# The five input combinations of a quad in three tiles instead of one

## The chip, the cores and the metric

The kernel runs on one core of a Trainium2 chip. The metric is device time in microseconds (us) of one execution, lower is better. Before the change the median of three runs is 695.69 us (686.91 to 696.82). One further execution was taken by the hardware profiler; all rows below come from it.

## What is computed

The reference is a StyleGAN-like stack of four modulated 1-D convolutions (kernel size 3, 64 channels in and out) on 128 samples of 64 channels and 1024 points, added to its input. Each sample has its own weights, modulated by its style vector:

```
s = style @ mw.T + mb
weight = SCALE * w * s[:, None, :, None]
demod = rsqrt(sum(weight * weight, axis=(2, 3)) + EPS)
weight = weight * demod[:, :, None, None]
```

The four layers are "same", "upsample" (transposed convolution with stride 2, then a blur), "same" and "downsample" (a blur, then a convolution with stride 2), each with a bias, and `x + layers(x)` is the result. There is no nonlinearity between the layers. So, away from the ends of a row, the four layers and the residual are one convolution per sample. The kernel builds those combined weights for each sample on the chip and applies them; the few points at the two ends of each row are computed separately.

## The kernel before

**Quads.** Four samples are one quad, and 32 quads are worked off in one unrolled loop (`for q in range(NQ)`). A sample fills 64 of the 128 partitions, so a quad is two pairs of samples. The row of 1024 points comes from memory as three planes (point numbers modulo 3), and the combined convolution is done by a Toom-Cook-like scheme: instead of nine products of weight taps with planes, five products, numbered 0 to 4, of five combinations of the weights with five combinations of the input. Each product is 24 matmuls of 64x64 weights with 340 points.

**Input side.** For each quad VectorE first makes `in3` (the combination for product 3, from the loaded planes X alone), then the helper tile G in three instructions (`in_g01` twice, `in_g2`). From G, GpSimd makes `in1` and `in2` (products 1 and 2), and VectorE makes `in04` (products 0 and 4, one instruction for each pair). All five combinations lie in one tile T, `[128, 2, 5, 344]` in f32, whose pool has two buffers; G has one buffer, X two.

**Weight side.** `stage1`, `stage2`, `stage3` are matmuls which chain the four layers' weights, with ScalarE scaling the results between them; `combine_a` and `combine_b` on VectorE make the weight combinations H.

**Products and sums.** `conv3`, `conv1` and `conv2` add up in one PSUM tile psA of the quad, and VectorE reads it between them: `sum1` (tile y) reads psA after conv1 and must be done before conv2 writes there; `sum2` reads it after conv2 and writes the PSUM tile Y, onto which `conv4` accumulates. `conv0` then accumulates onto psA. psA has two buffers, Y one. ScalarE turns the three sums into outputs (tile o), and SyncE's queue stores them.

**Order of the work.** The schedule is written by hand: each engine executes its instructions in the order in which the program records them. In iteration q the loop finishes quad q (conv4, conv0, outputs), does most products of quad n = q+1, and prepares the inputs and weights of c = q+2 and s = q+3. TensorE's order in an iteration is stage2(c), conv4(q), stage3(c) first part, conv3(n), stage3(c) second part, two thirds of conv0(q), in some iterations extra matmuls for the row ends (`slot`, tile psE), conv1(n), the last third of conv0(q), stage1(s), conv2(n). VectorE's order is sum2(q), combine_b(n), in04(n), in3(c), in_g01(c), in_g2(c), in some iterations extra small work (`extra`), sum1(n), more extra work, combine_a(c).

**Waits.** Waits are made by the framework. A new tile of a pool waits until every instruction that reads or writes the tile which held its buffer before is done. T(c) takes the buffer of T(q). The last reader of T(q) is the last third of conv0(q). The first writer of T(c) is `in3(c)` on VectorE.

The lines of the profile's rows: L494 is in3, L451 the helper for G, H, y and Y, L521 is in04, L509 and L514 are in1 and in2, L533 is the matmul of all products, L389 is stage2, L430 stage3, L358 stage1.

## Time and profile before

| what | value |
|---|---|
| median of three runs | 695.69 us (686.91 to 696.82) |
| the profiled execution, whole | 697.14 us |
| its span, first to last instruction | 695.3 us |
| TensorE matmuls (PE) busy | 540.5 us, 78% |
| VectorE (DVE) busy | 435.6 us, 63% |
| ScalarE (ACT) busy | 288.4 us, 41% |
| GpSimd (POOL) busy | 132.1 us, 19% |
| granted TensorE clock, mean | 0.904 |
| data moved by DMA | 70.32 MB, 101 GB/s on average |

Rows give start or busy time in us; "out<-in" names the tiles written and read; xN is the number of instructions. A bracket at the end of a timeline row is the engine's idle time just before it and what ended it. Busy shares are averages over the whole span.

### The profile page before, as it was taken

The numbers are of one execution on the slowest core, as the hardware profiler recorded it, in microseconds if no ns is written. First come the engines' busy times: TensorE is split into PE (matmuls) and PEld (weight loads), VectorE is DVE, ScalarE is ACT, GpSimd is POOL, SyncE is SP. The second block draws the span as 40 slices with busy tenths as digits, with TensorE's granted clock in tenths as the row PEclk, the third lists the DMA queues.
The fourth block names the chain that finished last, engine by engine and source line by source line (L and its number), as shares of the span: only waits on it lengthen the run. The fifth ranks groups of instructions, "written<-read, shape, count | busy, mean of one in ns | idle before, by whom it ended". The sixth has DMA issues, their size and how long they took to land.

```text
span 695.3 us, 20952 instructions
## 1 busy us (share of the span) xinstructions
PE 540.5 (78%) x9520; PEld 381.4 (55%) x9520; DVE 435.6 (63%) x632; ACT 288.4 (41%) x578; POOL 132.1 (19%) x142
## 2 busy tenths in 40 slices
PE   8976787788577866888886958887877786988875
PEld 6854555565456534655554645555555554656532
DVE  5666766647755576457756476646577666466772
ACT  4542444534254224424444324454334444444422
POOL 4123122122221012012212022210122211022220
PEclk9997999989899889899999889999899999899988
DMA  6124332234412332133422233312334323243113
GB/s 211 34 63 153 123 110 77 83 101 123 122 46 83 119 122 52 73 123 123 123 76 88 83 123 123 118 29 102 123 122 123 120 67 107 89 124 123 62 61 121
DMA packets 19720, 70.32 MB, mean 101 GB/s; under 512 B 2224, under 2 KB 2992, under 8 KB 19632
## 3 DMA queue, kind: packets, MB, share of 16 engines
q1 hardware_dynamic: 19552, 68.87, 31.2%
q8 instruction: 74, 1.21, 0.7%
q14 instruction: 14, 0.11, 0.1%
q10 hardware_dynamic: 80, 0.11, 0.0%
HBM read 35.36 MB, written 33.62 MB: 99 GB/s over the span
## 4 chain that ended last, share of the span: by engine, by line
PE 68%; DVE 25%; issue 4%; DMA 1%; ACT 1%; SPq 0%; DVEq 0%; ACTq 0%
PE psA L533 36%; PE psR L389 11%; PE psW L430 11%; DVE G L451 10%; PE Y L533 9%; DVE y L451 4%; DVE H L451 1%; PE psE L748 1%; DVE Wf L448 1%; DVE Ue L799 1%; DMA X<-in_x 1%; DVE Y L451 1%; DVE nw L237 1%; DVE Ve L764 1%; ACT o L587 1%
## 5 line engine op out<-in xcount | busy, mean ns | idle before, releaser
L533 PE MATMUL psA<-T,H 64*64 64x340 f32 x2304 | 221.4, 519 | 139.5 <-DVE y L451 138.7
L533 PEld LDWEIGHTS psA<-T,H 64*64 64x64 f32 x2304 | 103.4, 150 | 214.9 <-issue 143.9
L494 DVE TENSOR_TENSOR T<-X 128x684 f32<-128x684 f32 (+1 forms) x33 | 28.2, 854 | 201.8 <-PE psA L533 201.8
L509 POOL TENSOR_TENSOR T<-G 128x684 f32<-128x684 f32 x31 | 54.0, 1743 | 511.2 <-DVE G L451 511.2
L336 ACT ACTIVATE R<-psR,tC 128x448 f32<-128x448 f32 x63 | 36.6, 630 | 246.3 <-PE psR L389 241.6
L389 PEld LDWEIGHTS psR<-S,E 64*64 64x64 f32 x2304 | 94.1, 152 | 17.9 <-issue 11.7
L389 PE MATMUL psR<-S,E 64*64 64x192 f32 (+1 forms) x2304 | 99.9, 327 | 1.7 <-DVE S L338 1.3
L451 DVE SCALAR_TENSOR_TENSOR G<-X 128x688 f32<-128x688 f32 (+1 forms) x97 | 78.2, 860 | 0.7 <-DMA X<-in_x 0.7
L533 PE MATMUL Y<-T,Wf 64*64 64x340 f32 x768 | 64.0, 463 | 6.5 <-DVE Y L451 6.3
L533 PE MATMUL psA<-T,Wf 64*64 64x340 f32 x768 | 67.6, 447 | 0.0
L336 ACT ACTIVATE Wf<-psW,t 128x384 f32<-128x384 f32 (+1 forms) x126 | 56.3, 497 | 12.5 <-PE psW L430 12.5
L430 PE MATMUL psW<-R,w0s 64*64 64x128 f32 (+1 forms) x1536 | 61.3, 287 | 0.0
L514 POOL TENSOR_TENSOR T<-G 128x684 f32<-128x684 f32 x31 | 57.2, 1846 | 0.0
L587 ACT ACTIVATE o<-psA,tb,td 128x340 f32<-128x340 f32 x62 | 39.2, 634 | 41.9 <-PE psA L533 41.8
L430 PEld LDWEIGHTS psW<-R,w0s 64*64 64x64 f32 x1536 | 50.6, 133 | 7.6
L521 DVE TENSOR_TENSOR T<-G 128x684 f32<-128x684 f32 x64 | 54.1, 888 | 0.0
L587 ACT ACTIVATE o<-Y,tb,td 128x340 f32<-128x340 f32 x64 | 37.1, 630 | 32.2 <-ACT R L336 17.1
L451 DVE SCALAR_TENSOR_TENSOR H<-Wf 128x384 f32<-128x384 f32 x64 | 46.8, 731 | 0.0
L533 PEld LDWEIGHTS Y<-T,Wf 64*64 64x64 f32 x768 | 31.4, 137 | 26.2 <-DVE Y L451 6.1
L533 PEld LDWEIGHTS psA<-T,Wf 64*64 64x64 f32 x768 | 32.3, 134 | 16.0 <-issue 0.7
L451 DVE SCALAR_TENSOR_TENSOR Y<-m,psA 128x680 f32<-128x680 f32 x32 | 27.7, 866 | 21.1 <-PE psA L533 21.1
L587 ACT ACTIVATE o<-y,tb,td 128x340 f32<-128x340 f32 x63 | 38.7, 666 | 0.0
(136 smaller groups left out, 511.1 us busy)
## 6 DMA issues: line engine op xcount, KB each, us to landing
X<-in_x SPq DMA_DIRECT2D x64, 516.0 KB, 5.0
out<-o SPq DMA_DIRECT2D x62, 510.0 KB, 7.2
out<-o SPq DMA_DIRECT2D x2, 340.0 KB, 2.6
Xe<-in_x_ends SPq DMA_DIRECT2D x1, 512.0 KB, 9.8
par<-in_params SPq DMA_DIRECT2D x2, 192.0 KB, 3.4
out<-o SPq DMA_DIRECT2D x2, 170.0 KB, 3.3
par_s<-in_params_s SPq DMA_DIRECT2D x1, 196.0 KB, 2.8
par<-in_params SPq DMA_DIRECT2D x2, 96.0 KB, 2.9
```

The lines of the kernel that those rows point to most:

```text
L237: nc_v.scalar_tensor_tensor(n, n, -0.5, y, op0=ALU.mult, op1=ALU.mult)
L336: nc_a.activation(dst, src, AF.Copy, scale=f)
L389: nc.tensor.matmul(ps[r][cols, lo * C : (lo + m) * C], E[rows, e + 2, :], src[rows, a, :], start=(n == 0), stop=(n == 8), skip_group_check ...
L430: nc.tensor.matmul(ps[r][cols, at : at + m * C], w0s[kind][rows, k, :], rt[c][rows, first : first + K * (m - 1) + 1 : K, :], start=(n == 1 ...
L448: nc_v.scalar_tensor_tensor(v, idn3, t3[:, q, r : r + 1], v, op0=ALU.mult, op1=ALU.add)
L451: nc_v.scalar_tensor_tensor(out, x, f, y, op0=ALU.mult, op1=op)
L494: nc_v.tensor_sub(t[:, pairs, 4, :NJ], plane(X, 3, pairs), plane(X, 1, pairs))
L509: eng.tensor_add(t[:, :, 2, :NJ], plane(g, 2), plane(g, 1))
L514: eng.tensor_sub(t[:, :, 3, :NJ], plane(g, 2), plane(g, 1))
L521: nc_v.tensor_sub(t[:, c, 0:2, :NJ], both(a, PL), both(b, 1))
L533: nc.tensor.matmul(ps[cols, s, :NB], w, Ts[q][rows, c, SLOT[m], g : g + NB], start=(g == 0 and m == 3), stop=(g == K - 1), skip_group_chec ...
L587: nc_a.activation(dst, src, AF.Identity, bias=add, scale=d3)
```

## The change

The tile T becomes three: T3 for product 3 alone, T12 for products 1 and 2, T04 for products 0 and 4. Each has its own tag in the same pool, and so two buffers of its own; the sizes add up to the same memory. The tile G is now obtained apart from the T tiles. Matmuls read their operand from the tile that `SLOT` names. No instruction is added, removed or put at another place in any engine's order.

```diff
-    SLOT = {0: 0, 4: 1, 1: 2, 2: 3, 3: 4}
+    SLOT = {0: ("T04", 0), 4: ("T04", 1), 1: ("T12", 0), 2: ("T12", 1), 3: ("T3", 0)}
...
-    def t_tile(q):
-        if q not in Ts:
-            Ts[q] = tpool.tile([P, 2, 5, PL], F32, tag="T", name=f"T{q}")
+    def t_tile(q, tag):
+        if (q, tag) not in Ts:
+            Ts[q, tag] = tpool.tile([P, 2, 1 + (tag != "T3"), PL], F32, tag=tag, name=f"{tag}_{q}")
+        return Ts[q, tag]
+
+    def g_tile(q):
+        if q not in Gs:
             Gs[q] = gpool.tile([P, 2, 3 * PL], F32, tag="G", name=f"G{q}")
-        return Xs[q % NX], Ts[q], Gs[q]
+        return Xs[q % NX], Gs[q]

     def in3(q, pairs=BOTH_PAIRS):
         if q < NQ:
-            X, t, g = t_tile(q)
-            nc_v.tensor_sub(t[:, pairs, 4, :NJ], plane(X, 3, pairs), plane(X, 1, pairs))
+            X, t = Xs[q % NX], t_tile(q, "T3")
+            nc_v.tensor_sub(t[:, pairs, 0, :NJ], plane(X, 3, pairs), plane(X, 1, pairs))
...
     def in1(q, eng):
         if q < NQ:
-            X, t, g = t_tile(q)
-            eng.tensor_add(t[:, :, 2, :NJ], plane(g, 2), plane(g, 1))
+            t, g = t_tile(q, "T12"), Gs[q]
+            eng.tensor_add(t[:, :, 0, :NJ], plane(g, 2), plane(g, 1))
...
     def in04(q, c):
         if q < NQ:
-            X, t, g = t_tile(q)
+            t, g = t_tile(q, "T04"), Gs[q]
...
-            nc_v.tensor_sub(t[:, c, 0:2, :NJ], both(a, PL), both(b, 1))
+            nc_v.tensor_sub(t[:, c, :, :NJ], both(a, PL), both(b, 1))
...
     def product(q, m, ps, groups=range(K)):

         W, H_ = Wq[q]
+        tag, i = SLOT[m]
...
-                        Ts[q][rows, c, SLOT[m], g : g + NB],
+                        Ts[q, tag][rows, c, i, g : g + NB],
```

More of the change, by code (lines that the diff above doesn't have):

```diff
@@ L483, in plane @@
         return buf[:, pairs, at : at + NJ]
-    def t_tile(q):
-        if q not in Ts:
-            Ts[q] = tpool.tile([P, 2, 5, PL], F32, tag="T", name=f"T{q}")
+    def t_tile(q, tag):
[4 more added lines that the diff above has]
+        if q not in Gs:
             Gs[q] = gpool.tile([P, 2, 3 * PL], F32, tag="G", name=f"G{q}")
-        return Xs[q % NX], Ts[q], Gs[q]
+        return Xs[q % NX], Gs[q]
     def in3(q, pairs=BOTH_PAIRS):
         if q < NQ:
-            X, t, g = t_tile(q)
-            nc_v.tensor_sub(t[:, pairs, 4, :NJ], plane(X, 3, pairs), plane(X, 1, pairs))
+            X, t = Xs[q % NX], t_tile(q, "T3")
+            nc_v.tensor_sub(t[:, pairs, 0, :NJ], plane(X, 3, pairs), plane(X, 1, pairs))
     def in_g01(q, c):
         if q < NQ:
-            X, t, g = t_tile(q)
+            X, g = g_tile(q)
             sum_of(g[:, c, PL:], X[:, c, : 2 * PL], 0.5, X[:, c, PL:], ALU.subtract)
@@ L502, in in_g2 @@
         if q < NQ:
-            X, t, g = t_tile(q)
+            X, g = g_tile(q)
             sum_of(plane(g, 2, pairs), plane(X, 3, pairs), 0.5, plane(X, 2, pairs), ALU.subtract)
@@ L507, in in1 @@
         if q < NQ:
-            X, t, g = t_tile(q)
-            eng.tensor_add(t[:, :, 2, :NJ], plane(g, 2), plane(g, 1))
+            t, g = t_tile(q, "T12"), Gs[q]
+            eng.tensor_add(t[:, :, 0, :NJ], plane(g, 2), plane(g, 1))
     def in2(q, eng):
         if q < NQ:
-            X, t, g = t_tile(q)
-            eng.tensor_sub(t[:, :, 3, :NJ], plane(g, 2), plane(g, 1))
+            t, g = t_tile(q, "T12"), Gs[q]
+            eng.tensor_sub(t[:, :, 1, :NJ], plane(g, 2), plane(g, 1))
     def in04(q, c):
         if q < NQ:
-            X, t, g = t_tile(q)
+            t, g = t_tile(q, "T04"), Gs[q]
             a, b = g[:, c, :NJ], g[:, c, 2 * PL : 2 * PL + NJ]
             both = lambda v, step: bass.AP(v.tensor, v.offset, [list(v.ap[0]), [step, 2], [1, NJ]])
-            nc_v.tensor_sub(t[:, c, 0:2, :NJ], both(a, PL), both(b, 1))
+            nc_v.tensor_sub(t[:, c, :, :NJ], both(a, PL), both(b, 1))
     def product(q, m, ps, groups=range(K)):
         W, H_ = Wq[q]
+        tag, i = SLOT[m]
         for g in groups:
```

## The prediction

> **What bounds the kernel now.** I read the chain that ended last, then the costliest groups, then one quad in the timeline, then stretches with their clock. The chain first:

> ```profile
> PE 68%; DVE 25%; issue 4%; DMA 1%; ACT 1%; SPq 0%; DVEq 0%; ACTq 0%
> ```

> TensorE holds the end, but a quarter of the chain runs through VectorE, although that is busy only 63% of the span. The groups say where they meet (after the bar: busy time, mean ns, idle time before and what ended it):

> ```profile
> L533 PE MATMUL psA<-T,H 64*64 64x340 f32 x2304 | 221.4, 519 | 139.5 <-DVE y L451 138.7
> L494 DVE TENSOR_TENSOR T<-X 128x684 f32<-128x684 f32 (+1 forms) x33 | 28.2, 854 | 201.8 <-PE psA L533 201.8
> ```

> TensorE idles 138.7 us for y (sum1, before conv2). VectorE idles 201.8 us ahead of in3, for TensorE. Each waits for the other, once a quad. One quad without extra work, TensorE's timeline (start, duration, operation):

> ```profile
> 427.15 1.95 PE L533 MATMUL psA<-T,H 64*64 64x340 f32 x24 [3.23 <-DVE y L451]
> 428.88 2.71 PE L389 MATMUL psR<-S,E 64*64 64x192 f32 x72
> 431.68 1.95 PE L533 MATMUL Y<-T,Wf 64*64 64x340 f32 x24
> 433.44 0.94 PE L430 MATMUL psW<-R,par 64*64 64x192 f32 x24
> 434.20 0.94 PE L430 MATMUL psW<-R,w0s 64*64 64x128 f32 x24
> 434.96 1.90 PE L533 MATMUL psA<-T,H 64*64 64x340 f32 x24
> 436.68 0.94 PE L430 MATMUL psW<-R,w0s 64*64 64x128 f32 x24
> 437.44 1.32 PE L533 MATMUL psA<-T,Wf 64*64 64x340 f32 x16
> 438.59 1.89 PE L533 MATMUL psA<-T,H 64*64 64x340 f32 x24
> 440.30 0.75 PE L533 MATMUL psA<-T,Wf 64*64 64x340 f32 x8
> 440.87 1.15 PE L358 MATMUL psS<-wd,par 64*64 64x192 f32 x24
> 445.26 1.12 PE L533 MATMUL psA<-T,H 64*64 64x340 f32 x8 [3.24 <-DVE y L451]
> ```

> From conv2 (427.15) to the next conv2 (445.26) are 18.11 us: 14.87 us of work (to 442.02, the end of stage1) and 3.24 us of waiting. VectorE in the same quad:

> ```profile
> 433.96 1.65 DVE L521 TENSOR_TENSOR T<-G 128x684 f32<-128x684 f32 x2
> 441.12 0.87 DVE L494 TENSOR_TENSOR T<-X 128x684 f32<-128x684 f32 x1 [5.52 <-PE psA L533]
> 441.91 2.44 DVE L451 SCALAR_TENSOR_TENSOR G<-X 128x688 f32<-128x688 f32 x3
> 444.26 0.86 DVE L451 SCALAR_TENSOR_TENSOR y<-psA,m 128x680 f32<-128x680 f32 x1
> ```

> in04 ends at 435.61, and VectorE stands for 5.52 us until the last third of conv0 ends (441.05). Only then come in3, G and y, 4.0 us in a row, while TensorE has 1 us of stage1 left. Yet conv1, all that y needs from TensorE, ended at 440.48. Last, stretches (us; busy and count of each engine; PEclk is the granted clock):

> ```profile
> 58.12:666.74 608.62, 476.07 (x8489) 337.39 (x8489) 384.32 (x535) 255.59 (x505) 110.32 (x93) 0.91 0.32 102
> 427.15:445.26 18.11, 14.79 (x288) 10.21 (x289) 12.49 (x17) 8.68 (x17) 3.56 (x3) 1.00 0.38 118
> 445.20:449.00 3.80, 3.74 (x33) 2.43 (x37) 3.77 (x5) 0.00 (x0) 2.87 (x2) 0.55 0.90 237
> ```

> The pause costs twice. After it the clock is granted at 0.55 for some microseconds in most quads: conv2 at 445.26 took 3.39 us where the one at 427.15 took 1.95. The 29 quads between 58.12 and 666.74 hold 476.07 us of matmul work, where 29 at full clock would hold less (below).

> **The change part by part.**
> *The wait of in3 goes.* T3's buffer was last read by conv3(q), one iteration earlier; in the built program's list of waits in3 no longer waits for TensorE, and y does in its place, for conv1. T12's last reader is conv2(q) and T04's is conv0(q-1), both done when in1 and in04 come. So in3 and G move up into the idle 5.52 us: they end near 435.6 + 3.2 = 438.8, before conv1 ends.
> *What is late next:* y then waits for conv1 alone. From conv1's end: 0.07 us until VectorE starts (as in3 starts 0.07 after conv0), 0.86 for y, 0.14 until TensorE goes on (445.12 to 445.26): 1.07 us. TensorE has the last third of conv0 and stage1 to do meanwhile, 442.02 - 440.48 = 1.54 us. So y is covered with 0.47 us to spare, and a quad costs TensorE 14.87 us.
> *VectorE's demand:* 12.49 us in this quad. That holds 1.0 + 0.9 us by which H and Wf of combine_a are stretched beside in1 and in2 on POOL (H 1.55 against 0.55 elsewhere). POOL starts after G as before, but will now run while VectorE waits for conv1. 10.6 to 12.5 us fit into 14.87.
> *Other queues:* SyncE's loads wait for G, so they go out earlier; DMA moves 2.2 MB a quad (70.32 / 32), which in 14.87 us would be 148 GB/s, against 237 GB/s in the last row above. ScalarE needs 8.68 us of 14.87. The scaled S must be ready when stage2 starts: in the quad at 334.70 it took 0.97 us after stage1, which a conv2 of at least 1.7 us covers.
> *The clock:* without the pause nothing lets it fall. Its price is bounded: at worst all the dips stay (nothing gained), at best all go. I take the best, nearest to the rows of the quad 427.15 to 445.26, which held 1.00 while TensorE was busy.

> [...] Rows: a pause of 3.23 us was followed by full clock at 427.15 but by a conv2 of 3.04 us at 339.09. [...]

> **The sum,** against the profiled execution's span of 695.3.
> - 29 quads: 29 x 14.87 = 431.2. Row-end matmuls of psE: 9.9 for five large groups (2.1 + 1.8 + 1.6 + 2.8 + 1.6 busy), 2.5 estimated for the small ones.
> - Heavy quads: where VectorE does extra work its demand passes 14.87. Quad 117.79 to 141.41 had 17.38 busy, of which 1.3 is a stretched small instruction (oc, 1.55, against 0.25 in the first quad) that POOL will no longer meet: 16.1. Likewise 161.15 to 184.88: 17.53 less 1.3; 359.99 to 383.49: 17.15 less about 2. Together 2.8 above TensorE's time.
> - That is 446.4 in place of 608.62: 162.2 saved, of which some 131 are the waits and some 31 the clock.
> - First quad (31.60 to 58.12): in3 waits only 2.59 there, and G must wait for in2 of the quad before, until 48.7. About 2 saved. Last quads: warm matmuls and no stretched H, about 3.
> - Span 695.3 - 167.2 = 528; whole 1.84 more (697.14 - 695.3), 530. I add 2 for waits of a tenth of a microsecond that I can't see. **532 us.** The profiled execution stands 0.2% above the median, which changes nothing.

> **Rivals.**
> 1. *The clock doesn't recover* (short pauses remain, dips stay): 476.07 of busy work plus 5 for gaps, and 5 less at the ends, gives a span of 563 and a time of 565. For it: dips after 3.23 us. Against: after the change no pause of that size has a cause.
> 2. *VectorE becomes the bound*: if POOL goes on stretching it as now, each quad costs the larger of TensorE's time and VectorE's measured busy time (17.4, 17.5, 16.0, 17.2, 16.3 in the worst): some 456 for the 29 quads, 541 in all; with another 0.3 us a quad of waiting at Y, 550.
> 3. *The wait stays under another name*, for instance y waiting for its single buffer, freed by ScalarE's outputs: 697 if wholly. Against: in the quad before 339.09 those outputs end at 333.32 (332.10 + 1.22), a microsecond before conv1 does (332.41 + 1.90).
> 4. *Slower*: a gapless stream of matmuls is granted less clock for good. The limit where it decides: 14.87 / c exceeds today's 608.62 / 29 = 21.0 us a quad, so c below 0.71. At the 0.5 near which the dips lie, a quad costs 29.7 and the time is about 960. Against: 1.00 was held while TensorE was 14 us at work.

> **Chances.** Forecast 0.77, rivals 0.08 (1), 0.09 (2), 0.03 (3), 0.03 (4). The range reaches from 518 (no heavy quads, no small waits, some more at the first quad) to rival 1's 568. Faster by over 2% holds forecast and rivals 1 and 2: 0.94; the rest is split. About 2% is what a measurement of this kernel can tell from no change.

> **What would show it.** Right: in3 with no idle time before it, y idle for TensorE about 2 to 3 us a quad, the 138.7 us down to below 10, PEclk near 1.0, quads of 14.9 us, H of combine_a at 0.55. Wrong: conv2 still waits for y, conv4 waits for Y, stage2 waits for S on ScalarE, or a clock under 0.95 with TensorE busy throughout.

## The result, and the profile after

The changed kernel takes 512.61 us (median of four runs, 511.92 to 513.90); the kernel before took 693.58 us beside it (median of four, 686.91 to 696.82). The ratio is 0.7402, with a 95% interval of 0.7341 to 0.7463. The prediction was 532 us with a range of 518 to 568: the direction and the mechanism were right, and the time lies 5.4 us below the range. The profiled execution took 511.92 us, with a span of 510.0 us. (One of the four executions of the kernel with three buffers, below, took 1318.59 us, where the other three took 512 to 515; it is left out of the figures.)

The first view is the page of the changed kernel: the chain that ended last, then two groups (busy time, mean ns, idle time before and what ended it).

```profile
PE 81%; DVE 15%; issue 3%; ACT 1%; DVEq 0%; ACTq 0%
L538 PE MATMUL psA<-T,H 64*64 64x340 f32 x2304 | 187.5, 450 | 10.1 <-DVE y L451 10.1
L451 DVE SCALAR_TENSOR_TENSOR y<-psA,m 128x680 f32<-128x680 f32 x32 | 27.7, 866 | 72.5 <-PE psA L538 52.1
```

TensorE's share of the chain rose from 68% to 81%. Its idle time ahead of conv2 fell from 138.7 to 10.1 us, and VectorE now idles where the prediction put it, ahead of y, waiting for conv1. In the groups by shape, in3 (now L498) has no idle time before it at all:

```profile
L498 DVE TENSOR_TENSOR T<-X 128x684 f32<-128x684 f32 x31 | 28.3, 912 | 0.0
```

One quad without extra work, TensorE's timeline (start, duration, operation):

```profile
310.67 1.92 PE L538 MATMUL psA<-T,H 64*64 64x340 f32 x24
312.39 2.71 PE L389 MATMUL psR<-S,E 64*64 64x192 f32 x72
314.89 1.92 PE L538 MATMUL Y<-T,Wf 64*64 64x340 f32 x24
316.60 0.97 PE L430 MATMUL psW<-R,par 64*64 64x192 f32 x24
317.36 0.97 PE L430 MATMUL psW<-R,w0s 64*64 64x128 f32 x24
318.12 1.92 PE L538 MATMUL psA<-T,H 64*64 64x340 f32 x24
319.84 0.97 PE L430 MATMUL psW<-R,w0s 64*64 64x128 f32 x24
320.60 1.35 PE L538 MATMUL psA<-T,Wf 64*64 64x340 f32 x16
321.75 1.92 PE L538 MATMUL psA<-T,H 64*64 64x340 f32 x24
323.46 0.78 PE L538 MATMUL psA<-T,Wf 64*64 64x340 f32 x8
324.04 1.18 PE L358 MATMUL psS<-wd,par 64*64 64x192 f32 x24
325.01 0.78 PE L538 MATMUL psA<-T,H 64*64 64x340 f32 x8
```

From conv2 to conv2 are 14.34 us (310.67 to 325.01), without one bracket. The prediction built on 14.87. VectorE in the same quad:

```profile
315.86 1.65 DVE L525 TENSOR_TENSOR T<-G 128x684 f32<-128x684 f32 x2
317.42 0.87 DVE L498 TENSOR_TENSOR T<-X 128x684 f32<-128x684 f32 x1
318.20 2.44 DVE L451 SCALAR_TENSOR_TENSOR G<-X 128x688 f32<-128x688 f32 x3
323.80 0.87 DVE L451 SCALAR_TENSOR_TENSOR y<-psA,m 128x680 f32<-128x680 f32 x1 [3.15 <-PE psA L538]
324.58 0.55 DVE L451 SCALAR_TENSOR_TENSOR H<-Wf 128x384 f32<-128x384 f32 x1
```

in3 follows in04 at once. y starts 0.34 us after the last third of conv0 has begun (323.46) and ends at 324.67, 0.34 us before conv2 starts. H takes 0.55 us again. Last, the stretch of 29 quads (its length, busy time of PE, PEld, DVE, ACT and POOL, granted clock):

```profile
55.20:486.72 431.52, 428.29 (x8488) 335.02 (x8489) 342.51 (x535) 255.17 (x504) 108.82 (x94) 1.00 0.39 141
```

The same 29 quads took 608.62 us before, with 476.07 of matmul work at a clock of 0.91. Now the clock is 1.00, the work 428.29, and 3.2 us are idle.

### The profile page after: what moved, and what is told of

Its sections match the earlier page's. It is cut to its first block, busy times and chain, and to the rows that moved or that the text cites. A ratio compares the mean times of both kernels' runs of the same rounds, so it can differ in the third digit from the quotient of the medians.

```text
span 510.0 us, 20982 instructions
## 1 busy us (share of the span) xinstructions
PE 487.3 (96%) x9520; PEld 376.8 (74%) x9520; DVE 392.9 (77%) x632; ACT 288.7 (57%) x578; POOL 129.8 (25%) x142
## 2 busy tenths in 40 slices
DMA packets 19720, 70.32 MB, mean 138 GB/s; under 512 B 2224, under 2 KB 2992, under 8 KB 19632
## 4 chain that ended last, share of the span: by engine, by line
PE 81%; DVE 15%; issue 3%; ACT 1%; DVEq 0%; ACTq 0%
PE psA L538 37%; PE psR L389 14%; PE psW L430 12%; PE Y L538 9%; PE psS L358 5%; DVE G L451 3%; PE psE L753 2%; DVE T L525 2%; DVE H L451 2%; DVE y L451 2%; DVE nw L237 1%; ACT o L592 1%; DVE Y L451 1%; DVE Ue L804 1%; DVE y L574 1%
## 5 line engine op out<-in xcount | busy, mean ns | idle before, releaser
L538 PE MATMUL psA<-T,H 64*64 64x340 f32 x2304 | 187.5, 450 | 10.1 <-DVE y L451 10.1
L513 POOL TENSOR_TENSOR T<-G 128x684 f32<-128x684 f32 x31 | 54.3, 1751 | 332.6 <-PE psW L430 220.2
L389 PE MATMUL psR<-S,E 64*64 64x192 f32 (+1 forms) x2304 | 87.5, 299 | 0.6 <-ACT S L336 0.3
L389 PEld LDWEIGHTS psR<-S,E 64*64 64x64 f32 x2304 | 81.5, 133 | 7.7 <-DVE S L338 0.7
L451 DVE SCALAR_TENSOR_TENSOR y<-psA,m 128x680 f32<-128x680 f32 x32 | 27.7, 866 | 72.5 <-PE psA L538 52.1
L451 DVE SCALAR_TENSOR_TENSOR G<-X 128x688 f32<-128x688 f32 (+1 forms) x97 | 78.3, 860 | 0.5 <-DMA X<-in_x 0.5
L430 PE MATMUL psW<-R,w0s 64*64 64x128 f32 (+1 forms) x1536 | 62.7, 287 | 0.0
L430 PEld LDWEIGHTS psW<-R,w0s 64*64 64x64 f32 x1536 | 52.9, 133 | 6.1
L518 POOL TENSOR_TENSOR T<-G 128x684 f32<-128x684 f32 x31 | 53.2, 1716 | 0.0
L538 PEld LDWEIGHTS Y<-T,Wf 64*64 64x64 f32 x768 | 34.7, 134 | 18.6 <-issue 3.1
L538 PEld LDWEIGHTS psA<-T,Wf 64*64 64x64 f32 x768 | 35.0, 133 | 13.2
L451 DVE SCALAR_TENSOR_TENSOR Y<-m,psA 128x680 f32<-128x680 f32 x32 | 27.8, 870 | 16.3 <-PE psA L538 16.1
L358 PE MATMUL psS<-wd,par 64*64 64x192 f32 x768 | 38.9, 329 | 0.0
```

Source lines behind the costliest of these rows:

```text
L358: nc.tensor.matmul(ps[r][cols, k * C : (k + K) * C], woi[2][rows, k, :], src[rows, :], start=(k == 0), stop=(k == K - 1), skip_group_check ...
L389: nc.tensor.matmul(ps[r][cols, lo * C : (lo + m) * C], E[rows, e + 2, :], src[rows, a, :], start=(n == 0), stop=(n == 8), skip_group_check ...
L430: nc.tensor.matmul(ps[r][cols, at : at + m * C], w0s[kind][rows, k, :], rt[c][rows, first : first + K * (m - 1) + 1 : K, :], start=(n == 1 ...
L451: nc_v.scalar_tensor_tensor(out, x, f, y, op0=ALU.mult, op1=op)
L513: eng.tensor_add(t[:, :, 0, :NJ], plane(g, 2), plane(g, 1))
L518: eng.tensor_sub(t[:, :, 1, :NJ], plane(g, 2), plane(g, 1))
```

## The experiments

All times are medians; ratios stand against the kernel before, on the same chip and in the same hour.

**Which tile has to be apart?** Three kernels put the five combinations into two tiles, in three ways. Only `SLOT`, the sizes and the places inside the tiles differ from the change:

```diff
 # third apart
+    SLOT = {0: ("T0124", 0), 4: ("T0124", 1), 1: ("T0124", 2), 2: ("T0124", 3), 3: ("T3", 0)}
 # fourth and zeroth with third
+    SLOT = {0: ("T034", 0), 4: ("T034", 1), 1: ("T12", 0), 2: ("T12", 1), 3: ("T034", 2)}
 # zeroth and fourth apart
+    SLOT = {0: ("T04", 0), 4: ("T04", 1), 1: ("T123", 0), 2: ("T123", 1), 3: ("T123", 2)}
```

> Two tiles: products 3, 0 and 4 together, products 1 and 2 together. in3 again takes a buffer that conv0 read last. Theory: as before the change, 685 to 700, with some 200 us of idle time ahead of in3 and some 139 us ahead of conv2. Rival (any finer split frees part of the wait): below 660.

Measured: 694.00 us, ratio 0.9977 (0.9943 to 1.0011). The waits (in total, times, longest) are those of before:

```profile
DVE T L499 <- PE psA L539: 200.6, 30, 9.5
...
PE psA L539 <- DVE y L451: 137.2, 32, 7.4
```

As long as in3 shares a tile with what conv0 reads last, splitting gains nothing.

> Two tiles: products 0 and 4 together, products 1, 2 and 3 together. The buffer that in3 takes was read last by conv2 of the iteration before, which is long done. Theory: as after the change, 510 to 516; the third tile isn't needed. Rival: the wait for conv2 delays in3 by a microsecond a quad, 512 to 540.

Measured: 511.37 us, ratio 0.7359 (0.7329 to 0.7388), and quad for quad the times of the change, within 0.05 us. The third tile isn't needed; what counts is that conv0's operand lies apart from the others.

> Two tiles: the combination for product 3 alone, the other four together, two buffers each. in3 is free as after the change, but in1 and in2 on GpSimd now wait for the last third of conv0, so they run beside combine_a again. Theory (in3's wait is the whole gain, and 0.3 us of the quad of 14.87 us that the prediction was built on was conv4 waiting for a Y made late by GpSimd): the pause of about 138 us for y is gone, H is stretched to about 1.5 us again, a light quad costs about 14.6 us instead of 14.34, and the time is 516 to 526. Rival 1 (the split of T12 and T04 brings a good part): 560 or more. Rival 2 (GpSimd's place doesn't matter): 512 to 514, light quads 14.34.

Measured: 538.29 us, ratio 0.7755 (0.7725 to 0.7785). So in3's wait alone brings 157 of the 184 us that the version before it brought in the same hour. The rest hangs on GpSimd's place, more than I expected (516 to 526): from the start of stage2 to the start of conv4 the 29 quads take 23.9 us more in all than in the changed kernel, of 28.7 us between the two profiled executions. TensorE's light quad in this kernel:

```profile
324.53 1.90 PE L539 MATMUL psA<-T,H 64*64 64x340 f32 x24
326.24 2.68 PE L389 MATMUL psR<-S,E 64*64 64x192 f32 x72
329.17 1.95 PE L539 MATMUL Y<-T,Wf 64*64 64x340 f32 x24 [0.25 <-DVE Y L451]
...
338.37 1.15 PE L358 MATMUL psS<-wd,par 64*64 64x192 f32 x24
339.35 0.47 PE L539 MATMUL psA<-T,H 64*64 64x340 f32 x4
```

and VectorE's:

```profile
324.08 1.88 DVE L451 SCALAR_TENSOR_TENSOR H<-Wf 128x384 f32<-128x384 f32 x1
325.88 1.86 DVE L448 SCALAR_TENSOR_TENSOR Wf<-idn,t,Wf 128x64 f32<-128x64 f32 x2
...
328.25 0.87 DVE L451 SCALAR_TENSOR_TENSOR Y<-m,psA 128x680 f32<-128x680 f32 x1
```

in1 and in2 wait here for the last third of conv0, and so run on GpSimd beside combine_a. H takes 1.88 us in place of 0.55, the two Wf 1.86 in place of 0.47 (both 0.55 and 0.47 in the changed kernel's quad), so Y ends at 329.12, and conv4 starts 2.93 us after stage2 rather than 2.50. The quad costs 14.82 us. In quads with extra VectorE work behind sum1 that work is blocked too: most of them, where no row-end matmuls stand, cost 15.3 to 15.9 us, which my expectation had left out.

**Is it the tile or the buffer?**

```diff
-    tpool = ctx.enter_context(tc.tile_pool(name="tpool", bufs=2))
+    tpool = ctx.enter_context(tc.tile_pool(name="tpool", bufs=3))
```

> The kernel before, one tile of five combinations, but three buffers instead of two. in3 takes the buffer of quad c-3, whose conv0 is an iteration ago. Theory (only the age of the buffer's last reader counts, not the number of tiles): 510 to 516. Rival (separate tiles give something else, in waits or in memory placement): 530 or more.

> The kernel with one tile in three buffers once more, for its profile: 510 to 516, no idle time ahead of in3, light quads of 14.34 us.

Measured: 512.57 us (three executions, 512.16 to 515.28), ratio 0.7388 (0.7352 to 0.7425), and 512.06 us the second time, ratio 0.7368 (0.7346 to 0.7390). In the second run's profile a light quad takes 14.34 us, and in3 has no idle time ahead of it:

```profile
L494 DVE TENSOR_TENSOR T<-X 128x684 f32<-128x684 f32 x31 | 28.2, 911 | 0.0
```

One whole tile with a third buffer does what three tiles with two buffers do. The change is about the age of the buffer's last reader, not about tiles.

**Is it what stands behind the wait?** The kernel before, with in3 moved behind sum1, its wait unchanged; in a second version the loads stand behind in3.

```diff
-        in3(c)
...
         extra(q, 0)
         sum1(n)
+        in3(c)
+        load(c + NX)   # in the second version; in the first it stays ahead of sum1
```

> The kernel before, one tile with two buffers, but in3 stands behind sum1 in VectorE's order. Its wait for conv0 remains in the program; G and sum1 no longer stand behind it. Theory (the cost came from what was queued behind the wait): conv2's pause of 138 us is gone; but in3 and combine_a now run beside in1 and in2, so Y comes about 1.2 us late in a quad; 545 to 585. Rival (the tile itself must be free earlier): above 650.

In the first version in3 stands behind the load of quad c+2, so it combines that quad's planes: the same work on the wrong quad for product 3, and so a wrong result. Measured: 568.15 us, ratio 0.8185 (0.8146 to 0.8224). VectorE waited 43.8 us for loads of X, which the second version removes.

> As the kernel with in3 behind sum1, but the loads of the quad after next are recorded behind in3, so that in3 reads its own quad's planes and doesn't wait for a load. The result is the reference's again. Theory: the wait of 44 us for loads of X goes; what remains is in3 and combine_a beside in1 and in2 on GpSimd ahead of Y: 540 to 560. Rival (in3's own wait for conv0 costs even there): above 600.

Measured: 566.81 us, ratio 0.8155 (0.8133 to 0.8178), 6.8 us above the expectation. The wait for loads had hardly cost anything: a light quad takes 15.67 us without it and 15.82 with it. What remains shows in a light quad; VectorE's in3 and H, and then in another quad TensorE's conv4:

```profile
472.68 2.20 DVE L494 TENSOR_TENSOR T<-X 128x684 f32<-128x684 f32 x1
474.80 2.00 DVE L451 SCALAR_TENSOR_TENSOR H<-Wf 128x384 f32<-128x384 f32 x1
```

```profile
445.34 1.95 PE L533 MATMUL Y<-T,Wf 64*64 64x340 f32 x24 [1.11 <-DVE Y L451]
```

Without a tile or a buffer more, the order alone takes 18% off the time: sum1 no longer stands behind the wait. It stops at 567 because in3 and combine_a, all with two inputs in SBUF, now meet in1 and in2, and conv4 waits about 1.1 us for Y in each light quad and up to 2.8 us in others.

**What did the lower clock cost?** The kernel before, with matmuls of zeros in the place of the pause, so that TensorE stays at work while in3 waits as ever:

```diff
+        for i in range(fill):
+            for r, rows in enumerate(HALF):
+                for c, cols in enumerate(HALF):
+                    nc.tensor.matmul(
+                        ps[r][cols, : 5 * C], Z[rows, :C], Z[rows, : 5 * C],
+                        start=False, stop=(i == fill - 1), skip_group_check=True,
+                    )
...
-            stage1(s)
+            stage1(s, fill=FILL)   # FILL is 12, then 6
```

> The kernel before, with 48 matmuls of zeros added at the end of each stage1 of the loop, onto the PSUM tile of stage1, so that the sum is unchanged: about 3.2 us of TensorE work in the place of the pause ahead of conv2. in3 waits as before. Theory (the clock falls because of the pause): the idle time for y falls from 138 to about 45 us, most quads run at the full clock, and the time falls by 12 to 30 us although work was added: 665 to 683. Rival (the clock falls for another reason, and my 31 us belong elsewhere): 690 to 700.

Measured: 699.59 us, ratio 1.0076 (1.0042 to 1.0109), a clock of 0.992. I had mis-sized the filling; its records:

```profile
420.49 1.92 PE L546 MATMUL psA<-T,H 64*64 64x340 f32 x24
...
434.82 6.67 PE L371 MATMUL psS<-Z 64*64 64x320 f32 x96
441.28 1.93 PE L546 MATMUL psA<-T,H 64*64 64x340 f32 x24
```

Each f32 matmul of the program is two records, so 48 took 6.46 us (434.82 to 441.28), twice the pause. The time lies in the rival's range (690 to 700), because the filling was too long. The run is still of use: some 187 us of zeros were added (29 times 6.46) and the waiting for y fell from 138.7 to 10.2 us, and the time rose by only 5 us. From conv2 to conv2 a light quad takes 20.79 us, the zeros and 14.33 us: with the pause filled, everything else takes the changed kernel's time.

> As the filled kernel, with 24 matmuls of zeros instead of 48: the records of the filled kernel showed that 48 take 6.45 us, twice what was meant, so that they outlast the pause by 3.2 us in every light quad. 24 take 3.2 us, the length of a light pause. Theory (the clock falls because of the pause, and its price in the kernel before is about 31 us): clock above 0.96, light quads 18.1 us, 658 to 675. Rival (the price is nearer to nothing, or the clock falls again in the heavy quads, which keep 2 to 4 us of pause): 680 to 695.

Measured: 680.29 us, ratio 0.979 (0.9769 to 0.9811), a clock of 0.969 in the profiled execution. Useless work in the pause makes the kernel 15 us faster, and conv2 is slow (over 2.5 us in place of 1.95) in 8 of the 29 quads, where it was in 23 before and in none of the filled kernel. So the pause does lower the clock, and this has a price. The time lies in the rival's range, at its lower end, 5 us above mine, and what the rival named shows: heavy quads kept their pause, up to 4.2 us,

```profile
PE psA L546 <- DVE y L464: 45.3, 19, 4.2
```

and some dips with it. conv4's waits for Y also rose, from 6.3 to 12.8 us. This run shows at least 15 us; the size of the whole price is not shown by a run of its own and rests on the sum below.

**What is left in the changed kernel?** Of its 10.1 us of waiting for y, 6.2 fall in the first quad. Four rows of it, of VectorE, GpSimd, VectorE and TensorE:

```profile
45.44 2.31 DVE L498 TENSOR_TENSOR T<-X 128x684 f32<-128x684 f32 x1
...
50.24 1.63 POOL L513 TENSOR_TENSOR T<-G 128x684 f32<-128x684 f32 x1 [3.23 <-DVE G L451]
...
51.98 1.55 DVE L237 SCALAR_TENSOR_TENSOR nw<-nw,dm 128x64 f32<-128x64 f32 x1
...
55.20 3.49 PE L538 MATMUL psA<-T,H 64*64 64x340 f32 x24 [6.18 <-DVE y L451]
```

Small work on the tables (nw) stands ahead of sum1 and meets GpSimd's in1 and in2, so that an operation on 64 elements a partition takes 1.55 us. In five iterations this work can stand behind sum1:

```diff
+        late = q in (0, 4, 6, 15, 16)
+        if not late:
+            extra(q, 0)
         sum1(n)
+        if late:
+            extra(q, 0)
         extra(q, 1)
```

> The changed kernel, with the extra VectorE work of five iterations (0, 4, 6, 15, 16) moved from ahead of sum1 to behind it. Theory (what is left of waiting is this work standing ahead of sum1 while GpSimd blocks it): the pause of 6.2 us in the first iteration falls to about 3, the heavy quads of 15.0 to 16.1 us come to 14.5 to 15, and the time falls by 3 to 7 us. Rival (the same microseconds come back as a late Y ahead of conv4): within 1 us of the changed kernel.

> The changed kernel once more, as the mark for the next one: 510 to 514.

Measured: 504.63 us (503.86 to 505.51), ratio 0.7270 (0.7246 to 0.7295), beside 511.57 us (511.10 to 512.94), ratio 0.7376 (0.7352 to 0.7401), of the changed kernel. The waiting for y in total, times and longest is now

```profile
PE psA L538 <- DVE y L451: 3.3, 4, 2.0
```

and the intervals don't meet: 1.4% faster than the changed kernel, and the fastest version of this study.

## Why the prediction was right, and where it was wrong

**The wait of in3 goes: right.** The rows show it as predicted, and the runs with two tiles and with three buffers show that this wait, and not the number of tiles, carries it. Of the rivals, the clock that doesn't recover, the wait under another name and the slower clock did not come; nor did VectorE become the bound, outside the heavy quads that the sum had counted.

**What is late next, y: right.** It was worked out as 0.47 us to spare, with 0.14 us from y's end until TensorE goes on. The quad with y at 323.80 shows 0.34 us from y's end to conv2's start, so 0.20 by the same count: close, and on the right side.

**The clock: right in kind, its size only as a sum.** The 29 quads held 476.07 us of matmul work before. With 14.87 us a quad I had put 443.6 at the full clock, so 32 us to the clock. The filled kernels show that the pause causes the dips, and 15 us of their price directly. That "without the pause nothing lets it fall" held: the mean is 1.00 in the 29 quads, and the one dip in them stands behind the one long pause that is left (6.18 us, conv2 of 3.49).

**The sum: wrong, and by one term.** The step that failed is "a quad costs TensorE 14.87 us", taken from the quad at 427.15, which I held to be free of waiting except for its bracket. It was not. Measured from start to start, in that quad and in the one after the change: stage2 to conv4 2.80 against 2.50, conv4 1.76 against 1.71, stage1 1.15 against 0.97, the rest equal within 0.01. The first is a second wait, and the second goes with it: conv4's record is 1.95 us in the rows here where it waited, 1.92 after the change. VectorE's rows of that quad before the change, not shown then:

```profile
426.92 1.55 DVE L451 SCALAR_TENSOR_TENSOR H<-Wf 128x384 f32<-128x384 f32 x1
428.39 1.86 DVE L448 SCALAR_TENSOR_TENSOR Wf<-idn,t,Wf 128x64 f32<-128x64 f32 x2
...
430.76 0.86 DVE L451 SCALAR_TENSOR_TENSOR Y<-m,psA 128x680 f32<-128x680 f32 x1
```

Y ends at 431.62 and conv4 starts at 431.68: conv4 was waiting for Y, late because H and Wf were stretched beside in1 and in2. The row of conv4 has no bracket because stage2's record runs to 431.59, which leaves a gap of 0.09 us. I had counted that stretching as VectorE's demand, at 1.9 us a quad (too little: Wf alone is stretched by 1.4, 1.86 against 0.47, and VectorE's busy time fell from 12.49 to 10.21), and not followed it to the instruction that waits for Y. The run with the third tile apart puts in1 and in2 back beside combine_a, and its quad takes 14.82 us: the cost returns. The third difference, 0.18 us, is that I took stage1's end as the end of its work; the next matmul starts before that when nothing holds it (325.01, where stage1's record ends at 325.22).

So each light quad was put 0.53 us too high, 15.4 us in 29. With 14.34 the sum closes: 29 x 14.34 + 9.9 + 2.5 = 428.3, and the busy time measured is 428.29. That it closes so exactly is luck: from start to start the five large row-end groups add 9.2 us, not 9.9, and 1.6 us are the first conv2, still at the low clock (3.49 us).

**The other terms of the sum**, against the profiled execution: the 29 quads 431.5 us in place of 446.4 (14.9 less; the heavy quads and gaps hold the 3.2 us of idle time); the way to the first quad's conv2 1.7 less (29.93 in place of 31.60; the profiled execution of the split that gained nothing reached it at 29.13, so this isn't the change); the first quad 25.3 in place of 24.5; the end 23.3 in place of 25.6; and the 2 us added for waits that I couldn't see were not there. Together 20 us, from 532 to 512.

**The range** allowed for more waits and for a lost clock. It had no bound for the light quad itself, by which every other number was multiplied 29 times: its low end of 518 kept 14.87.

## What to carry to other kernels

An instruction that waits for a free buffer held up everything behind it in its engine's order. Where it was first to touch a tile, look for the last reader of the buffer it takes: a third buffer, a tile apart for what is read last, or another place in the order each removed most of the cost here (512, 511 and 567 of 695 us). When a pause goes, what ran beside it moves: follow a stretched instruction to whoever waits for its result, and take the length of a piece of matmul work from start to start in a stretch where nothing waits, not from the end of its record. A number that will be multiplied by the count of the loop deserves a second look, and bounds of its own.

## What the runs showed of the hardware

```profile
425.14:428.55 3.41, 1.40 (x20) 0.96 (x24) 3.41 (x5) 0.96 (x3) 2.16 (x2) 1.00 0.38 70
428.55:431.96 3.41, 3.33 (x84) 2.75 (x80) 3.38 (x5) 0.34 (x1) 1.41 (x1) 1.00 0.99 296
442.20:445.62 3.42, 0.36 (x7) 0.28 (x11) 3.42 (x5) 2.02 (x5) 1.11 (x1) 1.00 0.15 10
445.62:449.03 3.41, 3.41 (x33) 2.18 (x29) 3.38 (x5) 0.00 (x0) 2.45 (x2) 0.50 0.86 254
```

  The first pause falls across two intervals, and the clock stays; the second leaves 0.36 us of matmul work in one, and the next interval runs at 0.50. In the kernel before, conv2 was slow after each of the 23 pauses of which 2.26 us or more fell into one interval, and took 1.95 us after each of the 6 of which at most 2.01 us did. Of the 13 pauses of 3.15 to 3.25 us, 8 were followed by a slow conv2: which of them depended on where they lay in these intervals. The two microseconds are no sharp limit: in the fastest version a pause of 1.99 us in the first quad was followed by a conv2 of 3.18 us.
- Matmuls on zeros in the place of the pause held the clock up: 0.992 with 48 of them a quad and 0.969 with 24, in place of 0.904.
- In the profiles before and after the change, every operation of VectorE with two inputs in SBUF that began while GpSimd's in1 or in2 ran ended only after that one had, 0.03 to 0.73 us later, whatever its size: after the change in3 took 2.31 us in place of 0.87 (to 47.75, beside an in2 that ended at 47.01), and nw on 64 elements a partition 1.55 (to 53.53, in2 to 53.45). H took 1.88 in place of 0.55 with the third tile apart. y, with one input in PSUM, took at most 0.87 in both profiles, beside in1 too. The wait is inside the record's duration and shows as busy time, not as idle time: the row of nw has its 1.55 us and no bracket.
